# A decoder layer with a state-space scan: the products with C issued a step later, their consumers behind the next scan, the carries a step sooner

## The chip, the cores and the metric

The kernel runs on one core of a Trainium2 chip, in one launch. The metric is the device time of that core in microseconds, the median of a few runs. The engines are named as in the profile: PE multiplies matrices, DVE (VectorE) and ACT (ScalarE) work element by element, POOL is GpSimd, and SP only issues DMAs here.

## What is computed

One decoder layer on 8 sequences of 512 positions with 512 features: a Mamba block, an attention block on a second input, and a mixture of 32 experts, each followed by a residual and a layer norm. The part that the change touches is the Mamba block's recurrence. Cut to that part, the reference reads:

```python
xz = xn @ in_proj_w                                   # 512 -> 2 x 1024
x_main, z = jnp.split(xz, 2, axis=-1)
x_main = silu(causal_depthwise_conv1d(x_main))
dt, B_ssm, C_ssm = jnp.split(x_main @ x_proj_w, [32, 48], axis=-1)
dt = softplus(dt @ dt_proj_w + dt_proj_b)
dA  = exp(A * dt[..., None])                          # A = -exp(A_log), 1024 x 16 states
dBx = dt[..., None] * B_ssm * x_main[..., None]
h_t = dA_t * h_{t-1} + dBx_t                          # for every t, channel and state
y_t = sum over the 16 states of h_t * C_t
y   = (y + x_main * D_param) * silu(z)
out = res_scale * (y @ out_proj_w) + residual
```

After it come a layer norm, cross attention with 16 heads of 32 features, another norm, a router that picks 4 of 32 experts in groups, the experts with a capacity of 640 tokens each, a shared expert, a scatter-add and a last norm.

## The kernel before

**Stages.** `layers` does the Mamba and attention blocks, the routing and the shared expert; `experts` runs the 32 experts; `finish` does the last norm. The change lies in `layers`, which fills the profile up to about 3690 us.

**Chunks and steps.** The 8 sequences are cut into chunks of T = 256 positions, so there are 16 chunks, two to a sequence. A chunk has 32 steps, numbered k: four pairs q of blocks of 128 channels, and in each pair four groups g of 4 states, times the two blocks of the pair (ci). There are 512 steps in all. One step handles 128 channels, 4 states and 256 positions, laid out as a tile `h` of 128 x 4 x 257: the first column of each of the four stretches is the carry from the chunk before.

**What one step does.** `carry` (L452, ACT) takes a new `h` and copies the carries into it. `decays` (L446, ACT) makes the four 128x256 pieces of exp(A dt) in one of two buffers `das`, one step ahead. `scan` multiplies dt·x by B into `h` (L458, DVE), runs the recurrence in place (L462, DVE) and keeps the last column (L464, DVE). `collect` multiplies `h` by C in place (L479, DVE), and then PE sums over the states: four matmuls (L483) for each step into the PSUM tile `py`, behind two matmuls at the first group (L471) that put x·D there. When the 8 steps of a pair are done, `gated` (L495, DVE) multiplies `py` into silu(z).

**Buffers.** `h` has 4 buffers, so step k+4 reuses the memory of step k and has to wait until PE has read it. `py` has one. The broadcast rows of B and C come by DMA from a scratch tensor (`bcast`, six tiles `bc`). `prepare` makes dt and dt·x of the next pair: its last DVE instruction, L421, is followed by DMAs on SP's queue that spread the result into the tiles `both`, which the first L458 of the pair waits for.

**Work beside the scan.** In the same loop stand, at fixed k, the projection back of the chunk before (`back`, L512), the projection of z (`gate_x`, L311), its `silu` (L362, each with a change of ACT's function table), and for the next chunk the norm, the convolution (`convolve`, taps at L345), `x_proj` and `prepare`. The list `side` holds the attention, the routing and the shared expert of the sequence before, in pieces that are taken out as the planned work allows (`work`). Attention's scores (L775), their maxima (L777, DVE), the transposed scores (L801), the exponentials (L805, ACT) and the sums with V (L817) are the bulk of it.

**What sets the order.** No queue is written out by hand. Python traces the instructions in the loop's order, and the framework's scheduler then orders each engine's queue: among the instructions that its own model holds for ready it takes those traced first. The place of a call in the loop is thus a priority and not a position. Once a queue is built, its order is fixed. `do` and `settle` put the second part of a piece (the evacuation of its PSUM tile) behind the next piece.

The loop's lines around the change, before:

```python
h = carry(t, 2 * q + ci, g)
...
    decays(2 * nq + ni, ng, (f if k + 1 < len(steps) else nf)["ready", nq][0], das[(n + 1) % 2])
scan(t, 2 * q + ci, g, f["ready", q][1], bc, das[n % 2], h)
n += 1
if k % 8 == 0:
    if k:
        gated(q - 1, f, py)
...
settle()
collect(2 * q + ci, g, h, bc, py, f)
```

Of the kernel before, what the change touches and what calls it, by code (L numbers as in the profile page):

```python
# [8 lines left out]
F32 = mybir.dt.float32  # L9
# [3 lines left out]
ALU = mybir.AluOpType  # L13
# [4 lines left out]
P = 128  # L18
# [6 lines left out]
NST = 16  # L25
RANK = 32
CC = DI // P
T = 256
NT_ = T // P
NG = 4  # L30
HP = P // 2
# [51 lines left out]
def layers(ctx, tc, a, x1d, filld, based, xbuf):  # L83
# [23 lines left out]
    nc = tc.nc  # L107
# [11 lines left out]
    psy = ctx.enter_context(tc.tile_pool(name="l_psy", bufs=1, space=PSUM))  # L119
# [3 lines left out]
    ident = cp.tile([P, P], F32, name="l_ident")  # L123
    make_identity(nc, ident)

    twice = cp.tile([P, HP], F32, name="l_twice")
# [92 lines left out]
    first = cp.tile([P, E], F32, name="l_first")  # L219
    nc.gpsimd.iota(first, pattern=[[CAP, E]], base=-SLOTS, channel_multiplier=0, allow_small_or_imprecise_dtypes=True)  # L220
    first = first.unsqueeze(1).to_broadcast([P, SC, E])
# [158 lines left out]
    def bcast(f, g):  # L380

        got = []
        for r0 in (g * NG, NST + g * NG):
            t = bcp.tile([P, NG // 2, T], F32, tag="bc", name="bc")
            for r in range(2):
                n0 = r0 + r * NG // 2
                nc.sync.dma_start(
                    t[r * HP : (r + 1) * HP], f["scr"][n0 : n0 + NG // 2, :].partition_broadcast(HP)
                )
            got.append(t.unsqueeze(1).to_broadcast([P, 2, NG // 2, T]))  # L390
        return got
# [50 lines left out]
    def decays(c, g, dt, da):  # L442

        for n in range(NG):
            j, m = n // 2, n % 2
            nc.scalar.activation(da[:, n, 1:], dt[:, c % 2, j, :], AF.Exp, scale=aneg[:, c, j, g, m : m + 1])  # L446

    def carry(t, c, g):

        last = state[:, c, g].unsqueeze(2)  # L450
        h = mp.tile([P, NG, T + 1], F32, tag="h", name="h", bufs=4)
        nc.scalar.copy(h[:, :, 0:1], last if t else nothing)  # L452
        return h

    def scan(t, c, g, dtx, bc, da, h):

        steps = h.rearrange("p (j m) t -> p j m t", j=2)[:, :, :, 1:]
        nc.vector.tensor_tensor(  # L458
            steps, dtx[:, c % 2].unsqueeze(2).to_broadcast([P, 2, NG // 2, T]), bc[0], ALU.mult
        )  # L460
        flat = h.rearrange("p n t -> p (n t)")
        nc.vector.tensor_tensor_scan(flat, da.rearrange("p n t -> p (n t)"), flat, 0.0, ALU.mult, ALU.add)  # L462
        if t < S // T - 1:
            nc.vector.tensor_copy(state[:, c, g].unsqueeze(2), h[:, :, T : T + 1])  # L464

    def collect(c, g, h, bc, py, f):


        if g == 0:
            for j in range(2):  # L470
                nc.tensor.matmul(  # L471
                    py[j * HP : (j + 1) * HP, c % 2, :],
                    ident[:, j * HP : (j + 1) * HP],
                    f["xs"][c // 2][:, c % 2, :],
                    start=(c % 2 == 0),
                    stop=False,
                )
        steps = h.rearrange("p (j m) t -> p j m t", j=2)[:, :, :, 1:]
        nc.vector.tensor_tensor(steps, steps, bc[1], ALU.mult)  # L479
        for m in range(NG // 2):  # L480
            for j in range(2):
                s = (g, m, c % 2)
                nc.tensor.matmul(  # L483
                    py[j * HP : (j + 1) * HP, c % 2, :],
                    twice,
                    h[:, j * 2 + m, 1:],
                    start=False,
                    stop=(s == (NST // NG - 1, NG // 2 - 1, 1)),
                )

    def gated(q, f, py):

        f["xs"].pop(q)
        pair = f["zs"][:, 2 * q : 2 * q + 2, :]
        nc.vector.tensor_tensor(pair, pair, py, ALU.mult)  # L495

    def twice_x(b, t, f):
        f["o"] = o = mp.tile([P, NT_, D], F32, tag="xt", name="o")
        nc.sync.dma_start(o, a["x"][b, t * T : (t + 1) * T, :].rearrange("(j p) d -> p j d", p=P))
        nc.scalar.mul(o, o, 2.0)  # L500
# [501 lines left out]
    steps = [(q, g, i) for q in range(CC // 2) for g in range(NST // NG) for i in range(2)]  # L1002
    left = []

    def settle():

        got = [part() for part in left]
        left[:] = [x for x in got if x]

    def dry():  # L1010
        while left:
            settle()

    def do(fn, *args, first=False):

        if first:
            dry()
        rest = fn(*args)
        settle()
        if rest:  # L1020
            left.append(rest)

    def work(k):

        front = 6.9 if k in (1, 2) else 3.4 if 3 <= k < 7 or k in (12, 15, 18, 21, 24) else 1.0 if k in (11, 26) else 0.0
        return 1.2 + front

    f = {"xt": x0}
# [12 lines left out]
    bc, n = bcast(f, 0), 0  # L1041
    nc.scalar.activation(aneg, aneg, AF.Exp)
    nc.vector.tensor_scalar(aneg, aneg, -1.0, None, ALU.mult)
    decays(0, 0, f["ready", 0][0], das[0])
    old, side, cleared = None, [], 0

    for i, (b, t) in enumerate(chunks):
        nf = {}
        after = chunks[i + 1] if i + 1 < len(chunks) else None
        if t == 0:  # L1050
            side, spent = units(b - 1) if b else sources(0), 0.0

            own = [work(k) for k in range(len(steps))] * 2
            whole = sum(own) + sum(x[0] for x in side)
        py = None
        for k, (q, g, ci) in enumerate(steps):
            if ci == 0:
                if (q, g) != (CC // 2 - 1, NST // NG - 1):
                    bcn = bcast(f, (g + 1) % (NST // NG))
                else:  # L1060
                    bcn = bcast(nf, 0) if after else None
            h = carry(t, 2 * q + ci, g)

            if k + 1 < len(steps) or after:
                nq, ng, ni = steps[(k + 1) % len(steps)]
                decays(2 * nq + ni, ng, (f if k + 1 < len(steps) else nf)["ready", nq][0], das[(n + 1) % 2])
            scan(t, 2 * q + ci, g, f["ready", q][1], bc, das[n % 2], h)
            n += 1
            if k % 8 == 0:
                if k:  # L1070
                    gated(q - 1, f, py)
                elif old:
                    gated(CC // 2 - 1, old[2], old[3])
                py = psy.tile([P, 2, T], F32, tag="py", name="py")
            if i == 0 and k == 0:
                load("Wo")
            if i == 0 and k == 2:
                biases()
            if k == 0 and old:
                twice_x(*old[:3])  # L1080
            if k in (1, 2) and old:
                do(back, k - 1, *old[:3], first=True)
            if 3 <= k < 7:
                do(gate_x, k - 3, f, first=(k == 3))
            if k == 7:
                dry()
                silu(f["zs"])
            if k % 8 == 3:
                if q + 1 < CC // 2:
                    do(prepare, q + 1, f)  # L1090
                elif after:
                    do(prepare, 0, nf)
            if after:
                if k == 5:
                    load_x(*after, nf)
                if k == 9:
                    norm_x(nf)
                if k == 11:
                    for j in range(DC // 2):
                        do(flip_x, j, nf)  # L1100
                if k in (12, 15, 18, 21):
                    do(convolve, after[1], (k - 12) // 3, nf, first=(k == 12))
                if k == 23:
                    dry()
                    silu(*nf["xs"].values())
                if k == 24:
                    do(x_proj, nf)
            if side and (k >= 3 or t and k == 0):
                at = t * len(steps) + k + 1
                while side and spent + sum(own[:at]) <= whole * at / len(own):  # L1110
                    w, fn, alone = side.pop(0)
                    spent += w
                    do(fn, first=alone)
            settle()
            collect(2 * q + ci, g, h, bc, py, f)
            if ci == 1:
                bc = bcn
            while i < 2 and cleared < E * (i * len(steps) + k - 6) // (2 * len(steps) - 7):
                clear(cleared)
                cleared += 1  # L1120
        while t and side:
            _, fn, alone = side.pop(0)
            do(fn, first=alone)
        old = (b, t, f, py)
        f = nf
    gated(CC // 2 - 1, old[2], old[3])
    twice_x(*old[:3])
    for j in range(2):
        do(back, j, *old[:3], first=True)
    dry()  # L1130
    for _, fn, alone in units(B - 1):
        do(fn, first=alone)
# [347 lines left out]
```

## Time and profile before

| what | value |
|---|---|
| median of 3 runs | 5548.85 us (5548.56 to 5548.85) |
| the profiled execution: time, span | 5555.79 us, 5554.1 us |
| PE, DVE, ACT, POOL busy, share of the span | 88%, 78%, 47%, 10% |
| mean granted TensorE clock | 0.936 |
| steps of the scan | 512, from 54 to 3685 us |
| L462, the recurrence | 512 x 2291 ns |
| L458 and L479, the products with B and C | 512 x 1213 ns and 512 x 1218 ns |

The profiled execution took 5555.79 us, of which the instructions span 5554.1 us; it lies 6.9 us (0.12%) above the median. In the page's rows a line number is followed by the engine, the operation, the tile written and the tiles read, the number of instructions, the busy time in us with the mean of one in ns, and behind the second bar the time for which the engine stood idle just before such instructions, with the instruction that ended most of it. In the list of waits a row names who waited for whom, with the total in us, the number of waits and the longest.

### The profile page before, as it was taken

How to read it: one execution, taken by the hardware profiler on the slowest of the kernel's cores; microseconds unless marked ns; L12 is line 12 of the kernel's file. 1: busy time of each engine (PE TensorE's matmuls, PEld its weight loads, DVE VectorE, ACT ScalarE, POOL GpSimd, SP SyncE). 2: the span in 40 equal slices, each digit the busy share in tenths (PEclk: the TensorE clock that was granted, in tenths of full speed). 3: DMA queues.
4: the chain of work that ended last, by engine and by line, in shares of the span. 5: the costliest groups of instructions: out<-in, count | busy, mean ns of one | idle time of the engine just before them, and what ended most of it. 6: DMA issues, size and time to landing. Idle time of an engine off the chain costs nothing. (4 is left out here: it accounts for less than half of the span.)

```text
span 5554.1 us, 60352 instructions
## 1 busy us (share of the span) xinstructions
PE 4883.9 (88%) x19752; PEld 2720.5 (49%) x19752; DVE 4349.2 (78%) x5738; ACT 2592.8 (47%) x5483; POOL 560.9 (10%) x424
## 2 busy tenths in 40 slices
PE   6768889888988988888888898879899999999994
PEld 3334344334434434443443343333577777777773
DVE  7998989989889989899989999864466565555554
ACT  5554565655556555555555655523222222222223
POOL 1000002002000200200010020010111111111111
PEclk7878999999999999999999999989999999999997
DMA  6887345445534634544463464441345444454444
GB/s 183 246 239 203 108 130 184 114 120 154 167 104 113 203 92 129 184 123 113 124 199 104 114 193 110 113 157 44 102 121 125 125 125 124 121 126 124 115 121 146
DMA packets 554282, 769.83 MB, mean 139 GB/s; under 512 B 135754, under 2 KB 268394, under 8 KB 551920
## 3 DMA queue, kind: packets, MB, share of 16 engines
q1 hardware_dynamic: 517952, 677.55, 41.5%
q0 software_dynamic: 33280, 76.90, 7.3%
q10 hardware_dynamic: 2736, 11.54, 0.5%
q8 instruction: 156, 2.56, 0.2%
q14 instruction: 158, 1.29, 0.1%
HBM read 508.68 MB, written 165.05 MB: 121 GB/s over the span
## 5 line engine op out<-in xcount | busy, mean ns | idle before, releaser
L446 ACT ACTIVATE l_da<-both,l_aneg 128x256 f32<-128x256 f32 x2048 | 888.7, 499 | 791.5 <-DVE h L462 744.2
L462 DVE TENSOR_TENSOR_SCAN h<-l_da,h 128x1028 f32<-128x1028 f32 x512 | 1169.4, 2291 | 49.9 <-ACT h L452 27.3
L483 PE MATMUL py<-h,l_twice 128*64 128x256 f32 x4096 | 632.0, 424 | 194.2 <-DVE h L479 194.0
L458 DVE TENSOR_TENSOR h<-both,bc 128x1024 f32<-128x1024 f32 x512 | 617.5, 1213 | 141.8 <-PE py L483 78.2
L479 DVE TENSOR_TENSOR h<-h,bc 128x1024 f32<-128x1024 f32 x512 | 621.9, 1218 | 6.3 <-DMA l_qa<-l_ka 0.3
L483 PEld LDWEIGHTS py<-h,l_twice 128*64 128x64 f32 x4096 | 295.2, 148 | 570.5 <-issue 246.4
L775 PE MATMUL ps_s<-l_ka,l_qa 64*128 64x512 f32 x1024 | 315.2, 695 | 141.9 <-DVE mx L777 141.4
L1230 PE MATMUL ps_h<-xT,w 128*128 128x320 f32 x1536 | 435.6, 433 | 0.0
L1310 POOL DMA_INDIRECT based<-y,xe x160 | 251.2, 1570 | 1313.4 <-ACT y L1333 573.4
L1251 DVE TENSOR_TENSOR hT<-ps_h,p 128x320 f32<-128x320 f32 x128 | 62.9, 491 | 379.1 <-PE ps_h L1230 379.1
L777 DVE TENSOR_REDUCE mx<-ps_s 128x2 f32<-128x1024 f32 x256 | 310.2, 1215 | 56.2 <-PE ps_s L775 55.5
L1230 PEld LDWEIGHTS ps_h<-xT,w 128*128 128x128 f32 x1536 | 292.2, 190 | 118.2 <-issue 0.4
L801 PE MATMUL ps_t<-l_qa,l_ka 64*128 64x512 f32 x1024 | 300.6, 651 | 15.0 <-ACT eT L805 11.4
L805 ACT ACTIVATE eT<-ps_t 128x1024 f32<-128x1024 f32 x256 | 258.7, 1012 | 109.2 <-PE ps_t L801 108.7
L817 PE MATMUL po<-eT,l_va 128*64 128x512 f32 x1024 | 281.5, 628 | 24.6 <-ACT raw L829 20.8
L650 POOL DMA_INDIRECT xbuf<-x2t,dest x128 | 218.7, 1708 | 815.8 <-DVE dest L644 777.4
L1230 PE MATMUL ps_h<-t,s 128*128 128x320 f32 x1024 | 286.1, 432 | 0.0
L712 PE MATMUL ps_p<-x2T,wa 128*128 128x512 f32 x512 | 247.5, 633 | 11.8 <-DVE hT L892 10.3
L311 PE MATMUL ps_z<-xnT,wm 128*128 128x256 f32 x1024 | 241.0, 389 | 17.8 <-DVE o L521 17.0
L311 PE MATMUL ps_x<-xnT,wm 128*128 128x256 f32 x1024 | 242.5, 390 | 2.9 <-DMA wm<-in_in_proj_w 2.0
L512 PE MATMUL po<-wm,zs 128*128 128x512 f32 x512 | 234.6, 608 | 3.9 <-DMA wm<-in_out_proj_w 1.8
L1230 PEld LDWEIGHTS ps_h<-t,s 128*128 128x128 f32 x1024 | 194.6, 190 | 81.1
(234 smaller groups left out, 7414.6 us busy)
## 6 DMA issues: line engine op xcount, KB each, us to landing
bc<-scr SPq DMA_DIRECT2D x1024, 128.0 KB
w<-in_w SPq DMA_DIRECT2D x93, 1024.0 KB
wm<-in_in_proj_w SPq DMA_DIRECT2D x128, 512.0 KB
xbuf<-zero SPq DMA_DIRECT2D x32, 1362.5 KB
xe<-xbuf SPq DMA_DIRECT2D x32, 1362.5 KB
both<-dt SPq DMA_DIRECT2D x256, 128.0 KB
both<-dtx SPq DMA_DIRECT2D x256, 128.0 KB
wm<-in_out_proj_w SPq DMA_DIRECT2D x64, 512.0 KB
```

The lines of the kernel that those rows point to most:

```text
L311: nc.tensor.matmul(ps[:, i, :], w[:, dc, i * P : (i + 1) * P], f["xnT"][:, dc, :], start=(dc == 0), stop=(dc == DC - 1),)
L446: nc.scalar.activation(da[:, n, 1:], dt[:, c % 2, j, :], AF.Exp, scale=aneg[:, c, j, g, m : m + 1])
L458: nc.vector.tensor_tensor(steps, dtx[:, c % 2].unsqueeze(2).to_broadcast([P, 2, NG // 2, T]), bc[0], ALU.mult)
L462: nc.vector.tensor_tensor_scan(flat, da.rearrange("p n t -> p (n t)"), flat, 0.0, ALU.mult, ALU.add)
L479: nc.vector.tensor_tensor(steps, steps, bc[1], ALU.mult)
L483: nc.tensor.matmul(py[j * HP : (j + 1) * HP, c % 2, :], twice, h[:, j * 2 + m, 1:], start=False, stop=(s == (NST // NG - 1, NG // 2 - 1, 1)),)
L775: nc.tensor.matmul(ps[:, j, :], qa[r, lt * P : (lt + 1) * P], ka[r, :], start=True, stop=True)
L777: return lambda: nc.vector.tensor_reduce(mx[:, lt, :].unsqueeze(2), ps, AX.X, ALU.max) and None
L801: nc.tensor.matmul(ps[:, j, :], ka[r, kc * P : (kc + 1) * P], qa[r, :], start=True, stop=True)
L805: nc.scalar.activation(eT, ps, AF.Exp)
L817: nc.tensor.matmul(po[j * 2 * HD : (j + 1) * 2 * HD, :], va[:, kc, i, j * HD : (j + 2) * HD], eT[:, j, :], start=(kc == 0), stop=(kc == SC ...
L1230: nc.tensor.matmul(ps, w[:, n, r * P : (r + 1) * P], x[:, n, :], start=not more and n == 0, stop=n == 1, skip_group_check=more,)
```

## The change

`collect` now does only the multiplication with C (L469) and returns a function `products`, which the loop calls one step later, ahead of the next step's `collect`. With it goes the allocation of `py`, which the first products of a pair now make. `carry` of step k+1 is called in step k, ahead of the decays of step k+1. `gated` moves from the first to the second step of the next pair, `back` from k = 1, 2 to 2, 3, `gate_x` from 3..6 to 4..7, the `silu` of z from 7 to 8, and `side` may begin a step later. A `settle` is called right behind the scan and its consumers, in place of the one just ahead of `collect`. After the last chunk the last `products` are called ahead of the last `gated`. Nothing else is changed: same tiles, same buffers, same instructions, apart from what the scheduler makes of them. In the new file L489 are the products, L479 the two x·D matmuls, L469 the multiplication with C and L503 `gated`.

```diff
-    def collect(c, g, h, bc, py, f):
-        if g == 0:
-            for j in range(2):
-                nc.tensor.matmul(py[...], ident[...], f["xs"][c // 2][:, c % 2, :], ...)
+    def collect(c, g, h, bc, f):
         steps = h.rearrange("p (j m) t -> p j m t", j=2)[:, :, :, 1:]
         nc.vector.tensor_tensor(steps, steps, bc[1], ALU.mult)
-        for m in range(NG // 2):
-            for j in range(2):
-                nc.tensor.matmul(py[...], twice, h[:, j * 2 + m, 1:], ...)
+        xs = f["xs"][c // 2]
+
+        def products():
+            if g == 0 and c % 2 == 0:
+                f["py"] = psy.tile([P, 2, T], F32, tag="py", name="py")
+            py = f["py"]
+            if g == 0:
+                for j in range(2):
+                    nc.tensor.matmul(py[...], ident[...], xs[:, c % 2, :], ...)
+            for m in range(NG // 2):
+                for j in range(2):
+                    nc.tensor.matmul(py[...], twice, h[:, j * 2 + m, 1:], ...)
+
+        return products
...
-            h = carry(t, 2 * q + ci, g)
+            h = ahead
             if k + 1 < len(steps) or after:
                 nq, ng, ni = steps[(k + 1) % len(steps)]
+                ahead = carry(t if k + 1 < len(steps) else after[1], 2 * nq + ni, ng)
                 decays(2 * nq + ni, ng, ...)
             scan(t, 2 * q + ci, g, f["ready", q][1], bc, das[n % 2], h)
             n += 1
-            if k % 8 == 0:
-                if k:
-                    gated(q - 1, f, py)
+            if k % 8 == 1:
+                if k > 1:
+                    gated(q - 1, f)
                 elif old:
-                    gated(CC // 2 - 1, old[2], old[3])
-                py = psy.tile([P, 2, T], F32, tag="py", name="py")
+                    gated(CC // 2 - 1, old[2])
...
-            if k in (1, 2) and old:
-                do(back, k - 1, *old[:3], first=True)
-            if 3 <= k < 7:
-                do(gate_x, k - 3, f, first=(k == 3))
-            if k == 7:
+            settle()
+            if k in (2, 3) and old:
+                do(back, k - 2, *old, first=True)
+            if 4 <= k < 8:
+                do(gate_x, k - 4, f, first=(k == 4))
+            if k == 8:
                 dry()
                 silu(f["zs"])
...
-            if side and (k >= 3 or t and k == 0):
+            if side and (k >= 4 or t and k < 2):
...
-            settle()
-            collect(2 * q + ci, g, h, bc, py, f)
+            if products:
+                products()
+            products = collect(2 * q + ci, g, h, bc, f)
```

More of the change, by code (lines that the diff above doesn't have):

```diff
@@ L464, in scan, with gated @@
             nc.vector.tensor_copy(state[:, c, g].unsqueeze(2), h[:, :, T : T + 1])
-    def collect(c, g, h, bc, py, f):
-        if g == 0:
-            for j in range(2):
[L471 to L477, printed above, removed]
+    def collect(c, g, h, bc, f):
         steps = h.rearrange("p (j m) t -> p j m t", j=2)[:, :, :, 1:]
         nc.vector.tensor_tensor(steps, steps, bc[1], ALU.mult)
-        for m in range(NG // 2):
-            for j in range(2):
[L482 to L491, printed above, removed]
+        xs = f["xs"][c // 2]
[5 more added lines that the diff above has]
+                for j in range(2):
+                    nc.tensor.matmul(
+                        py[j * HP : (j + 1) * HP, c % 2, :],
+                        ident[:, j * HP : (j + 1) * HP],
+                        xs[:, c % 2, :],
+                        start=(c % 2 == 0),
+                        stop=False,
+                    )
+            for m in range(NG // 2):
+                for j in range(2):
+                    s = (g, m, c % 2)
+                    nc.tensor.matmul(
+                        py[j * HP : (j + 1) * HP, c % 2, :],
+                        twice,
+                        h[:, j * 2 + m, 1:],
+                        start=False,
+                        stop=(s == (NST // NG - 1, NG // 2 - 1, 1)),
+                    )
+        return products
+    def gated(q, f):
         f["xs"].pop(q)
         pair = f["zs"][:, 2 * q : 2 * q + 2, :]
-        nc.vector.tensor_tensor(pair, pair, py, ALU.mult)
+        nc.vector.tensor_tensor(pair, pair, f["py"], ALU.mult)
     def twice_x(b, t, f):
@@ L1023, in work @@
     def work(k):
-        front = 6.9 if k in (1, 2) else 3.4 if 3 <= k < 7 or k in (12, 15, 18, 21, 24) else 1.0 if k in (11, 26) else 0.0
+        front = 6.9 if k in (2, 3) else 3.4 if 4 <= k < 8 or k in (12, 15, 18, 21, 24) else 1.0 if k in (11, 26) else 0.0
         return 1.2 + front
@@ L1044, in layers @@
     decays(0, 0, f["ready", 0][0], das[0])
+    ahead, products = carry(0, 0, 0), None
     old, side, cleared = None, [], 0
@@ L1054, in layers @@
             whole = sum(own) + sum(x[0] for x in side)
-        py = None
         for k, (q, g, ci) in enumerate(steps):
@@ L1079, in layers @@
             if k == 0 and old:
-                twice_x(*old[:3])
-            if k in (1, 2) and old:
-                do(back, k - 1, *old[:3], first=True)
-            if 3 <= k < 7:
-                do(gate_x, k - 3, f, first=(k == 3))
-            if k == 7:
+                twice_x(*old)
+            settle()
[4 more added lines that the diff above has]
+            if k == 8:
                 dry()
@@ L1123, in layers @@
             do(fn, first=alone)
-        old = (b, t, f, py)
+        old = (b, t, f)
         f = nf
-    gated(CC // 2 - 1, old[2], old[3])
-    twice_x(*old[:3])
+    products()
+    gated(CC // 2 - 1, old[2])
+    twice_x(*old)
     for j in range(2):
-        do(back, j, *old[:3], first=True)
+        do(back, j, *old, first=True)
     dry()
```

## The prediction

> **What bounds the kernel now.** I read the page's table of engines first, then a window over the steady part of the scan, then the list of waits, then the order of time around one wait.
>
> ```profile
> PE 4883.9 (88%) x19752; PEld 2720.5 (49%) x19752; DVE 4349.2 (78%) x5738; ACT 2592.8 (47%) x5483; POOL 560.9 (10%) x424
> 139.00:3600.00 3461.00, 2972.29 (x12178) 1411.87 (x12178) 3142.33 (x3570) 1963.59 (x4174) 259.60 (x189) 0.93 0.51 148
> ```
>
> The second line (length; then busy time of PE, PE's loads, DVE, ACT, POOL) is the stage that the change touches. DVE is busy for 3142.3 of 3461 us, 91%, so 319 us is all that better order could give there. PE shows 86% and ACT 57%. What ends DVE's idle time, and whom PE's products keep waiting:
>
> ```profile
> DVE h L458 <- PE py L483: 78.2, 33, 5.2
> DVE h L458 <- DMA both<-dtx: 47.9, 21, 6.9
> DVE xs L345 <- ACT xs L337: 43.7, 25, 9.8
> DVE h L462 <- ACT h L452: 27.3, 15, 2.0
> DVE zs L495 <- PE py L483: 23.9, 17, 2.4
> PE py L483 <- DVE h L479: 194.0, 58, 9.1
> ACT h L452 <- PE py L483: 199.4, 137, 6.9
> ```
>
> The largest idle time of DVE in the scan is L458 waiting for products: the buffer of `h` that step k+4 wants is still being read for step k. One such place in order of time:
>
> ```profile
> 2418.97 7.03 PE L712 MATMUL ps_p<-x1T,wa 128*128 128x512 f32 x16
> ...
> 2425.93 1.08 PE L483 MATMUL py<-h,l_twice 128*64 128x256 f32 x8
> ...
> 2427.06 1.23 DVE L458 TENSOR_TENSOR h<-both,bc 128x1024 f32<-128x1024 f32 x1 [3.42 <-PE py L483]
> ```
>
> PE's queue holds 7 us of attention's projections ahead of the products; the products follow at 2425.93 and DVE, which has stood for 3.42 us, goes on as they end. So the products are not late because their input is late: they are late because of what is queued ahead of them.
>
> **What the Trainium skill says.** "Perfetto Trace Analysis", section Optimization Strategy, says that the same gap coming back on the engine that should be saturated can mean too few buffers. The trace agrees: this wait of 3 to 5 us comes back at the same two steps in every pair of chunks (at 2338.8 and 2427.1 us, and 469 us earlier at 1870.0 and 1956.7). The section on the Tensor Engine Instruction of that page says that DVE and ACT are strict FIFO: whatever stands behind a waiting L458 or a waiting carry waits too; the 3.42 us above is bare idle time. "ScalarE: Activation LUTs", section What ACT_TABLE_LOAD costs, gives 1283 ns for a load and 1380 ns for a drain with it; the trace has 1283 ns, and 1.0 us of idle time before the 61 loads of L362 together, so I price a load at 1.28 us alone.
>
> **The change, part by part.** No matmul, DMA or vector instruction of the loop is added or taken away. The order of the built queues, before and after, tells what the scheduler does with the new places.
>
> *Products a step later.* Each is traced behind the next step's scan and side work, so PE's queue puts more ahead of them. I counted for each of the first 508 steps how many multiplications with C of later steps PE's queue needs done before it gets to this step's products: none, one, two, three. Before: 205, 167, 129, 7. After: 209, 124, 155, 20. Two or more rise from 136 to 175, with four buffers as before. What that costs, as an estimate from the trace's durations: take the last DVE instruction that PE's queue needs up to step k's products, the DVE work from there to L458 of step k+4 (rows: 1.213, 2.291, 1.218 us, 1.215 for L777, others by their size), and subtract PE's work from the same point through the products (intervals between back-to-back matmuls: 0.29 us a product, 0.46 a 128x256, 0.96 a 128x512, 0.55 an attention matmul). Where this is below zero the buffer can't be free in time. Before, 27 steps are, 34.1 us in sum, and the trace has 19 of its waits and 57 of its 78.2 us just there, so the count finds the places. After, 75 are, 79.7 us in sum. The ratio is 2.34. Of neighbouring steps only the worst should pay, since a stall also gives PE time: with one payment for adjacent steps it is 57.1 over 31.5, 1.81; with one for steps up to four apart 48.0 over 31.5, 1.52. I take 1.81: 78.2 us become 141.5, **+63 us**, between +41 and +105. Most of it should stand in one run of steps, the second to seventh of the second chunk of a sequence, where `back` and `gate_x` sit on PE.
>
> *Less waiting on PE.* What the move could bring is the 194 us in which the products stand at the head of PE's queue waiting for L479, with attention behind them. But the steps whose own multiplication is the latest thing PE needs are 128 before and 130 after. I take **0**; the bounds are -60 (a third of it, if it all reached DVE) and 0.
>
> *Carries a step sooner.* They need the same buffer, which now comes free later. Carries that stand ahead of their own step's decays on ACT rise from 151 to 181, and behind a waiting carry ACT's decays, exponentials and evacuations wait. ACT is idle for 43% of the stage, which hides most. I scale L462's wait for it, 27.3 us, by 181/151: **+5**, between -27 (all of it gone) and +25.
>
> *dt·x of the next pair.* The scheduler, not an edit, moves L421 further ahead of the pair's first L458. At the second pair of a chunk the DVE work between them, 1.3 us before, becomes 5.0 and 1.2 in turn; at the third 5.0 and 7.8 become 8.0 and 13.9; at the fourth 8.7 and 5.7 become 12.6 and 9.0. In order of time the 47.9 us split into 30.1 at the second pair, 6.8, 6.9 and 4.1 at the others. Half of the first and both of the next go: **-29**, between -44 and 0. SP's queue issues the same DMAs and isn't waited for.
>
> *`gated` a step later*, on DVE behind the next scan: its wait of 23.9 us gets some 5 us more for the last products, which are themselves later. **-10**, between -24 and +5. The next pair's first products wait for it on PE (`py` is one buffer; L471 waits 14.9 us now): both move by one step, 0, between -15 and +10.
>
> *`back`, `gate_x`, `silu`, `side` a step later.* Same work; `silu` stays one step ahead of its reader. Loads of ACT's tables fall from 138 to 98, 40 x 1.28 = 51 us, since the scheduler no longer splits the silu calls around an exponential. ACT isn't full, so what shows is L462's wait for decays (8.3 us) and the taps' (43.7): **-5**, between -25 and 0. The first chunk and the tail after the last one see the same instructions: 0; were its cover gone, a step's products are 1.1 us.
>
> The sum is 63 + 0 + 5 - 29 - 10 - 5 = +24 us, 0.43%. On the profiled execution, 5555.8 us, that is 5580; it stood 6.9 us above the median, and on the median of 5548.85 it is **5573 us**.
>
> **The rivals.** (a) *The products' full price.* DVE pays every deficit (+105), and the carries, held by the same buffers, stop ACT for another 25: with 15 us left of the gains, +115 us, 5664. For it speaks that ACT's carries already wait 199.4 us for PE; against it that stalls relieve each other. (b) *Faster: PE runs free.* The 194 us on PE's queue shrink. The counts of what DVE owes to PE go that way for other matmuls: the scores' matmuls (L775), which wait for the maxima (141.4 us of PE's idle time), are pressed in 80 places instead of 126 by the same kind of count. If PE gains about 60 us through this, its deficits of 1 us a step dissolve: the products' extra +63 doesn't come, and with -29, -10, -5 and some -15 of the old 78.2 us it is -59, 5490. It decides when PE is ahead by more than a microsecond at most of the 75 places; against it stand the 128 and 130. (c) *The change doesn't do what it says.* The scheduler re-forms nearly the same queues, the counts are scatter, gains and losses cancel: 5549.
>
> **How the numbers follow.** The measurement can tell about 0.2%, 11 us, from no change. The forecast, slower by some 24 us (its own range 5562 to 5612), has a chance of 0.43; rival (a) 0.10; (b) 0.31; (c) 0.16. So faster 0.31, same 0.16, slower 0.53. The range reaches from (b) to short of (a): 5490 to 5645.
>
> **What would show it.** Right: L458's wait for the products (L489) grows from 78 us to 110 to 180 and stands at more steps; its wait for `both` falls under 30 us; ACT shows 98 loads; DVE's busy time in the scan is unchanged and its idle time grows. Wrong: L458's wait is at or under 78 us, or PE's wait of products for L469 falls far under 194 us and the scores' with it, and the scan ends before 3690 us. An equal time with a smaller buffer wait would mean that another wait took its place, ACT's carries first.

## The result and the profile after

The changed kernel takes 5606.39 us (median of 4 runs, 5602.28 to 5612.04) against 5548.85: 57.5 us more, a ratio of 1.0102 with a 95% interval of 1.0085 to 1.0120. The direction was forecast, at less than half the size (24 us). The profiled execution took 5602.28 us with a span of 5600.6, 46.5 us over the span of before. It is the shortest of the four runs while the profiled one of before lay above its median, so the traces hold 46.5 of the 57.5 us.

The page's engine line and the same window of the scan as before (length; busy PE, PE's loads, DVE, ACT, POOL):

```profile
PE 4884.3 (87%) x19752; PEld 2727.5 (49%) x19752; DVE 4358.2 (78%) x5738; ACT 2535.0 (45%) x5443; POOL 541.5 (10%) x424
139.00:3600.00 3461.00, 2926.92 (x11960) 1400.62 (x11962) 3101.95 (x3533) 1873.12 (x4065) 238.53 (x189) 0.93 0.51 146
```

The work of the whole kernel is the same for PE and DVE; in the window DVE is busy for 3102 us instead of 3142 and so idle for 359 instead of 319, and PE does 45 us less there. Taken step by step, the last recurrence starts at 3736.3 us instead of 3680.6: 55.7 us are lost inside the scan, and the part behind it is 9.2 us shorter: DVE has 29 instructions, 7.4 us, less to do there, so some of that work is now done earlier. ACT has 40 instructions less, the table loads that fell from 138 to 98 as counted.

The list of DVE's waits after (who for whom: us in total, times, longest):

```profile
DVE h L458 <- PE py L489: 108.8, 77, 5.3
DVE mx L785 <- PE ps_s L783: 76.1, 47, 2.8
...
DVE xs L345 <- ACT xs L337: 49.1, 34, 10.7
DVE h L458 <- DMA both<-dtx: 39.0, 9, 8.6
...
DVE h L462 <- ACT h L452: 31.6, 20, 3.9
DVE g_m L567 <- ACT g_sc L566: 27.7, 7, 5.4
...
DVE zs L503 <- ACT zs L362: 17.2, 6, 2.9
...
DVE zs L503 <- PE py L489: 10.1, 5, 3.0
```

And from the list of all waits, what ACT and PE waited for:

```profile
ACT h L452 <- PE py L489: 247.7, 129, 11.5
...
PE py L489 <- DVE h L469: 189.9, 57, 8.9
PE ps_s L783 <- DVE mx L785: 187.5, 92, 4.8
```

No single row holds 57 us. The wait for products rose by 30.6 us (78.2 to 108.8), the maxima's wait for the scores by 20.6 (55.5 to 76.1), a wait for the router's exponential is all but new (0.4 to 27.7), `gated` waits 9.0 more for silu (8.2 to 17.2) and 13.8 less for products (23.9 to 10.1), the wait for dt·x fell by 8.9 (47.9 to 39.0). PE's waits for the multiplication with C are what they were (194.0 and 189.9).

### The profile page after: what moved, and what is told of

Read it like the earlier page. It is cut to its first block, busy times and chain, and to the rows that moved or that the text cites. A ratio compares the mean times of both kernels' runs of the same rounds, so it can differ in the third digit from the quotient of the medians.

```text
span 5600.6 us, 60350 instructions
## 1 busy us (share of the span) xinstructions
PE 4884.3 (87%) x19752; PEld 2727.5 (49%) x19752; DVE 4358.2 (78%) x5738; ACT 2535.0 (45%) x5443; POOL 541.5 (10%) x424
## 3 DMA queue, kind: packets, MB, share of 16 engines
q14 instruction: 159, 1.29, 0.1%
## 5 line engine op out<-in xcount | busy, mean ns | idle before, releaser
L462 DVE TENSOR_TENSOR_SCAN h<-l_da,h 128x1028 f32<-128x1028 f32 x512 | 1168.8, 2292 | 50.9 <-ACT h L452 31.6
L489 PE MATMUL py<-h,l_twice 128*64 128x256 f32 x4096 | 656.0, 427 | 189.9 <-DVE h L469 189.9
L458 DVE TENSOR_TENSOR h<-both,bc 128x1024 f32<-128x1024 f32 x512 | 618.6, 1216 | 154.7 <-PE py L489 108.8
L469 DVE TENSOR_TENSOR h<-h,bc 128x1024 f32<-128x1024 f32 x512 | 621.7, 1218 | 6.8
L489 PEld LDWEIGHTS py<-h,l_twice 128*64 128x64 f32 x4096 | 303.4, 148 | 559.6 <-issue 233.5
L783 PE MATMUL ps_s<-l_ka,l_qa 64*128 64x512 f32 x1024 | 306.4, 665 | 187.9 <-DVE mx L785 187.5
L785 DVE TENSOR_REDUCE mx<-ps_s 128x2 f32<-128x1024 f32 x256 | 310.5, 1216 | 77.5 <-PE ps_s L783 76.1
L658 POOL DMA_INDIRECT xbuf<-x2t,dest x128 | 205.8, 1608 | 782.0 <-DVE dest L652 697.1
L783 PEld LDWEIGHTS ps_s<-l_ka,l_qa 64*128 64x128 f32 x1024 | 85.2, 191 | 343.0 <-DVE mx L785 281.2
```

Of the source, the lines that this page charges most:

```text
L458: nc.vector.tensor_tensor(steps, dtx[:, c % 2].unsqueeze(2).to_broadcast([P, 2, NG // 2, T]), bc[0], ALU.mult)
L489: nc.tensor.matmul(py[j * HP : (j + 1) * HP, c % 2, :], twice, h[:, j * 2 + m, 1:], start=False, stop=(s == (NST // NG - 1, NG // 2 - 1, 1)),)
L783: nc.tensor.matmul(ps[:, j, :], qa[r, lt * P : (lt + 1) * P], ka[r, :], start=True, stop=True)
L785: return lambda: nc.vector.tensor_reduce(mx[:, lt, :].unsqueeze(2), ps, AX.X, ALU.max) and None
```

## The experiments

**Products alone: nothing to run.** A kernel of before in which only the products are issued a step later (behind the next scan, ahead of `gated`) was built. Its queues are those of before on every engine, instruction by instruction: the scheduler puts the products where it put them already. So at that place the first clause of the change does nothing, and its effect needn't be measured. In the changed kernel the products stand further back in the loop, ahead of the next `collect` and so behind that step's pieces; that place by itself, with the `gated` that it forces a step later, was not measured.

**Carries alone.** `carry_only` is the kernel before with one edit:

```diff
-            h = carry(t, 2 * q + ci, g)
+            h = ahead
...
+                ahead = carry(t if k + 1 < len(steps) else after[1], 2 * nq + ni, ng)
                 decays(...)
```

> The kernel before with the carries alone a step sooner. PE's queue stays as it was; only ACT's order changes, at 328 places. Theory A (buffers of h, of which the sooner carries are a part): L462's wait for carries grows from 27 us by about 5, time +5 us (0.1%). Theory B (the moved consumers make the loss): no change that can be measured, within 0.2%. Theory C (carries that wait for a buffer hold up ACT's exponentials): +20 us or more, with L462's wait for L452 at 50 us or over.

Measured 5555.7 us, ratio 1.0007 [1.0000, 1.0014]; DVE's wait for the carries is 23.5 us. The other way round, the changed kernel without this edit:

> The changed kernel with the carries back at their own step. Theory A and B: within 0.2% of the changed kernel, 5595 to 5615 us, L462's wait for carries at 25 to 35 us. Theory C (carries): 20 us or more faster than the changed kernel.

Measured 5603.93 us, ratio 1.0101 [1.0084, 1.0118], the time of the changed kernel; the wait for carries falls to 7.5 us and the wait for products rises to 134.2. The 24.1 us that go from the one wait come back as 25.4 in the other: the carries decide in which row the waiting shows, and they don't set the time. Theory C falls.

**The moved consumers alone.** `consumers_only` moves `back`, `gate_x`, `side` and the settle, and leaves products, `gated`, silu and carries. With the pieces goes their weight in `work`, the plan by which `side` is dealt out; the changed kernel has that shift too, though the diff further up leaves the line out:

```diff
-            if k in (1, 2) and old:
-                do(back, k - 1, ...)
-            if 3 <= k < 7:
-                do(gate_x, k - 3, ...)
+            settle()
+            if k in (2, 3) and old:
+                do(back, k - 2, ...)
+            if 4 <= k < 8:
+                do(gate_x, k - 4, ...)
...
-            if side and (k >= 3 or t and k == 0):
+            if side and (k >= 4 or t and k < 2):
...
-            settle()
             collect(...)
```

> The kernel before with only back, gate_x and side a step later (and the settle behind the scan); products, gated, silu and carries stay where they were. Theory A (the products' own delay makes the loss): within 0.3% of before. Theory B (the moved consumers): the larger part of the +57 us of the whole change, 30 us or more, with new waits of DVE for the router's exponential (L566 of the changed kernel; about 27 us) and for the scores, and the wait of L458 for products over 78 us at the steps just behind the moved pieces.

Measured 5661.86 us, 1.0205 [1.0188, 1.0222]: about twice the loss of the whole change. Theory B holds on the time, but not in its detail: the wait for the router isn't there and the wait for products is at its old size (75.0 us); what grew most is the wait for dt·x, which was 47.9 us:

```profile
DVE h L458 <- DMA both<-dtx: 93.6, 20, 8.9
```

The carries set no time, so the other edits of the change (products, `gated` and silu a step later) take away about 55 us of what the moved consumers cost. Which of the three does so was not tried; together they are a gain beside the moved pieces, where the prediction had its largest loss.

**A fifth buffer.** `after_h5` is the changed kernel with `bufs=5` for `h`; the router's `g_any`, `g_gs` and `g_rank` share memory with its other tiles to make room.

> The changed kernel with five buffers of h in place of four; three small router tiles share memory to make room. Theory A (buffers are what L458 waits for): its wait for products falls from 109 us under 40 us and the time falls by 40 us or more, near or below the kernel before. Rival: the scheduler uses the fifth buffer to put still more ahead of the products (steps whose products stand behind three or more later multiplications rise from 20 to 144), so the wait stays near 100 us and the time within 20 us of the changed kernel.

Measured 5606.18 us, 1.0098 [1.0081, 1.0115], equal to the changed kernel. DVE's two largest waits of L458:

```profile
DVE h L458 <- DMA both<-dtx: 107.8, 19, 8.8
DVE h L458 <- PE py L489: 95.0, 56, 4.4
```

The rival holds: the wait for products stays near 100 us, the one for dt·x grows from 39.0 to 107.8, and the time is the same. Theory A, which is the prediction's view that the loss is one of buffers of `h`, is not borne out. The scheduler made new queues for five buffers; what a fifth would do in unchanged queues isn't shown.

**Which consumer.** Three kernels move one piece each, on the kernel before: `back` alone, `gate_x` alone (each with its weights in `work`), the settle alone; and one is the changed kernel with `back` at its old k = 1, 2.

> The kernel before with back alone a step later (k = 2, 3), with its weights in the plan. Theory D (back is the piece whose move costs, since its 16 matmuls now come together with prepare of the next pair and stand ahead of products): +25 us or more, with more waits of L458 for products or for both. Theory E (no single piece: gate_x, side and back cost only together): within 0.3% of before.

> The kernel before with gate_x alone a step later (k = 4 to 7), with its weights in the plan. Theory D (back is the piece): within 0.3% of before, L458's wait for products at or under 78 us. Rival (gate_x is the piece, behind prepare of the next pair): +25 us or more, with L458's wait for both over 80 us.

> The kernel before with only the settle moved from just ahead of collect to just behind the scan's consumers. ACT's table loads fall from 138 to 87, 65 us of ACT. Theory (ACT is off the path): within 0.2% of before. Rival (ACT's order holds DVE up at silu and the taps): 15 us or more faster. Theory E' (the settle makes the loss of consumers_only): 25 us or more slower.

> The changed kernel with back at its old steps, k = 1, 2. Theory D (back): the loss is gone for the most part, 5550 to 5580 us. Theory E (the pieces cost together, or another one carries it): within 0.3% of the changed kernel, 5590 to 5620 us.

Measured: `back_only` 5618.53 us, 1.0121 [1.0104, 1.0138]; `gate_only` 5556.47, 1.0006 [0.9997, 1.0014]; `settle_only` 5586.42, 1.0054 [1.0037, 1.0071]; `after_back` 5571.38, 1.0035 [1.0022, 1.0047]. So theory D holds for the most part: `back` costs, and `gate_x` doesn't. About a third of the changed kernel's loss is left when `back` is put back, and the settle alone costs about half as much as the whole change, in spite of 51 table loads less (138 to 87), which bring nothing that shows. In `after_back` only the call of `back` moves; the plan in `work` and the steps that are closed to `side` (k = 2, 3) stay as in the changed kernel. With `back` at its old place the wait for products is less than half of what it was in the changed kernel:

```profile
DVE mx L785 <- PE ps_s L783: 94.5, 61, 3.2
...
DVE h L458 <- PE py L489: 50.1, 59, 6.3
```

**Both put back, and the four combinations.** `after_settle` is the changed kernel with the settle ahead of the products again, `after_back_settle`, whose edit is shown, has `back` at k = 1, 2 as well:

```diff
-            settle()
-            if k in (2, 3) and old:
-                do(back, k - 2, *old, first=True)
+            if k in (1, 2) and old:
+                do(back, k - 1, *old, first=True)
...
+            settle()
             if products:
                 products()
```

> The changed kernel with back at its old steps and the settle at its old place. If the settle carries what is left of the loss (it cost 33 us alone), the time falls from 5571 to 5540 to 5560 us, level with the kernel before; if not, it stays within 0.3% of 5571.

> The changed kernel with only the settle at its old place. If settle and back add up, 30 us under the changed kernel, 5565 to 5585 us, and DVE's wait for the router's exponential is gone; if settle costs only in company with back's old place, within 0.2% of 5606.

| changed kernel, ratio to before | `back` at 2, 3 | `back` at 1, 2 |
|---|---|---|
| settle behind the scan's consumers | 1.0102 [1.0085, 1.0120] | 1.0035 [1.0022, 1.0047] |
| settle ahead of the products | 1.0046 [1.0028, 1.0064] | 0.9973 [0.9963, 0.9984] |

`back`'s place costs 0.67% in one row and 0.73% in the other, the settle's 0.56% and 0.62%: they add up, to 1.29%, and everything else in the change gains 0.27% (0.16 to 0.37). `after_back_settle`, at 5541.62 us, is faster than both kernels; its products are a step later, and L458 waits for them for 53.1 us, less than the 78.2 of before.

These prices hold in the changed kernel. In the kernel before, `back` alone costs 1.21%, and it does so by other waits:

```profile
DVE h L458 <- PE py L483: 99.5, 66, 3.9
DVE xs L345 <- ACT xs L337: 97.9, 39, 9.2
```

The convolution's taps wait for ACT 54 us longer there than before (43.7), and the wait that the account below is about isn't there: at the fifth and sixth steps of the second chunks L458 waits for no products at all. Why the move of `back` alone does that is open; what follows holds for the changed kernel.

**Why `back` costs there.** First the changed kernel in order of time, at one of those places (start, length, engine, line, tiles; in brackets the idle time and what ended it):

```profile
2111.01 1.22 DVE L785 TENSOR_REDUCE mx<-ps_s 128x2 f32<-128x1024 f32 x1
...
2112.34 7.13 PE L520 MATMUL po<-wm,zs 128*128 128x512 f32 x16
...
2112.46 1.23 DVE L458 TENSOR_TENSOR h<-both,bc 128x1024 f32<-128x1024 f32 x1 [0.22 <-PE py L489]
...
2113.79 2.30 DVE L462 TENSOR_TENSOR_SCAN h<-l_da,h 128x1028 f32<-128x1028 f32 x1
...
2116.12 1.23 DVE L469 TENSOR_TENSOR h<-h,bc 128x1024 f32<-128x1024 f32 x1
...
2119.89 1.03 PE L489 MATMUL py<-h,l_twice 128*64 128x256 f32 x8
2120.85 0.70 PE L520 MATMUL po<-wm,zs 128*128 128x512 f32 x1
...
2120.97 1.22 DVE L458 TENSOR_TENSOR h<-both,bc 128x1024 f32<-128x1024 f32 x1 [3.62 <-PE py L489]
```

A half of `back` is 7.13 us on PE. In the step beside it DVE has its own L458, L462 and L469 and nothing else, done 4.9 us after they began; then it stands for 3.62 us until PE has done the half and the products behind it. The next half follows at 2120.85. With `back` a step earlier, in `after_back`, the first half runs beside attention's work on DVE:

```profile
2089.27 7.13 PE L520 MATMUL po<-wm,zs 128*128 128x512 f32 x16
...
2089.98 0.69 DVE L856 TENSOR_TENSOR total<-total,r 128x512 f32<-128x512 f32 x1
...
2090.70 0.69 DVE L857 SCALAR_TENSOR_TENSOR total<-total,r 128x512 f32<-128x512 f32 x1
...
2091.43 0.69 DVE L858 SCALAR_TENSOR_TENSOR attT<-attT,total 128x512 f32<-128x512 f32 x1
...
2092.04 0.68 DVE L503 TENSOR_TENSOR zs<-zs,py 128x512 f32<-128x512 f32 x1
...
2092.64 1.22 DVE L458 TENSOR_TENSOR h<-both,bc 128x1024 f32<-128x1024 f32 x1
```

Here DVE has L856 to L858 and `gated` (L503) beside its scan for the time in which PE is taken up, and its L458 starts without a wait. In the kernel before, the queues put the same pieces of attention (there L848 to L850) beside the first half, and the wait behind it is short:

```profile
2081.60 7.13 PE L512 MATMUL po<-wm,zs 128*128 128x512 f32 x16
...
2082.26 0.69 DVE L848 TENSOR_TENSOR total<-total,r 128x512 f32<-128x512 f32 x1 [0.56 <-ACT r L847]
...
2090.23 1.22 DVE L458 TENSOR_TENSOR h<-both,bc 128x1024 f32<-128x1024 f32 x1 [1.03 <-PE py L483]
```

The place shown is one of seven, one in each second chunk from the second sequence on, always at the sixth step (k = 5). These seven waits sum to 28.2 us in the changed kernel, 3.5 before and nothing in `after_back`. Two more places follow `back`: the fifth step of the same chunks has 8.6 us (1.6 in `after_back`), and the eighth step of the first chunks 32.2 (13.8). Of the 53.6 us that so go, 18.4 come back as the maxima's wait for the scores (76.1 to 94.5); the times differ by 35.

The reading was tested by making the halves shorter, with the places kept. Both kernels leave out half of the matmuls:

```diff
-                for i in range(2):
+                for i in range(1):
                     c = 2 * q + i
                     nc.tensor.matmul(pos[j], yg[:, c, ...], w[:, i, :], ...)
```

> The kernel before with half of back's matmuls left out (8 of 16 in a chunk; the projection back then sums only half of the channels). It is the measure for the next kernel. PE loses 113 us of work; if PE is not the bound where back stands before, the time falls by under 25 us (the waits for products just behind back, 24 us).

> The changed kernel with the same half of back's matmuls left out. Theory F (back's 7.1 us halves are longer than the DVE work of the steps where they stand now, so PE sets the pace there): the loss against the same kernel before shrinks from 57 us to under 25 us, and L458's wait for products falls from 109 us under 60 us. Rival (what was moved upsets the order as such, however long the matmuls are): the loss stays at 40 us or more.

Measured 5509.29 us for the kernel before (0.9923 [0.9907, 0.9940]) and 5522.04 for the changed one (0.9947 [0.9930, 0.9964]): 12.8 us apart where the full kernels are 57.5. The wait for products is 47.3 and 52.8 us. At the place that was shown, DVE has the same three instructions beside the shorter half, and its wait behind it is a quarter of what it was:

```profile
2078.07 4.43 PE L520 MATMUL po<-wm,zs 128*128 128x512 f32 x8
...
2084.00 1.23 DVE L458 TENSOR_TENSOR h<-both,bc 128x1024 f32<-128x1024 f32 x1 [0.92 <-PE py L489]
```

The seven waits of the sixth step fall from 28.2 to 3.3 us. So theory F holds: at these places it is the length of `back` on PE against the DVE work beside it. Whether as much PE work taken away elsewhere would have brought the two kernels as near to each other was not tried. The expectation for the kernel before missed: it gained 46 us (0.77%; the kernel before stood at 5555.45 us beside it), not under 25, so PE sets the pace in places there too.

**What the settle costs.** In the changed kernel, the wait that comes with the moved settle and goes with the old one is DVE's for the router's exponential (27.7 us, and 0.4 in `after_settle`). Two kernels tried it alone, and one both edits with it:

> The changed kernel with the router's work behind its exponential as a part of its own, behind the next piece. If that wait (27 us) is on the path, the time falls by 15 to 30 us and the rest of the settle's cost is small; if it covers another wait, the time stays within 0.2% of 5606.

> The changed kernel without the router's exponential (its scores are then ranked as plain differences, so other experts are picked; the sizes of all work stay the same). Theory (the wait for it is on the path and is the settle's part of the loss): DVE's 27 us wait is gone and the time falls by 18 to 30 us against the changed kernel, to 5576 to 5590 us. Rival (it covers other waits): within 0.2% of 5606 us, with L458's and the scores' waits grown by some 25 us.

> The same, and the router's work behind its exponential becomes a part of its own, behind the next piece. Theory (DVE's 24 us of waiting for that exponential are on the path): that wait is gone and the time is 10 to 25 us under that of the kernel without this edit. Rival (the wait covers another one, PE's): it goes, and waits for the scores grow by as much, the time the same within 0.2%.

Measured 5602.49 us (1.0094 [1.0076, 1.0113]), 5599.21 us (1.0090 [1.0073, 1.0107]) and 5538.31 us (0.9973 [0.9961, 0.9986]). In `after_router` the wait stayed in the queue (25.6 us in the scan), so that run tells nothing of it; in `after_back_settle` it was gone (0.4 us) before the edit was made, so the third doesn't either. In `after_noexp` it is gone, and 15.3 us of waiting for PE (L899, which takes up the result of a projection) are new; the gain against the changed kernel, some 7 us, is not clear of its interval. Nor can that wait be the settle's price everywhere: `settle_only` is 0.54% slower with 0.4 us of it. There it is `gated`'s wait for the products that grew most, from 23.9 us:

```profile
DVE zs L495 <- PE py L483: 51.6, 23, 4.4
```

The settle's cost is shown as an edit; by which wait it reaches the time stays open.

## Why the prediction was wrong in size

**What held.** The kernel became slower, and the wait for products grew where it was said to: in the second to seventh step of a sequence's second chunk the order of time has 51.7 us after 15.3, and that is more than the whole growth. The reading that the products are late for what PE's queue holds ahead of them, and not for their input, holds too. The carries were put at +5 us, and `carry_only` measured 0.07%, 4 us, with [0.00, 0.14]%. PE's wait for the multiplication with C was put at no gain: 194.0 became 189.9. Loads of tables fell to 98. Rival (b) is out, since the kernel is slower; its sign fails as well: the scores' waits on PE rose, 141.4 to 187.5 us, where its count had let them fall.

**That the direction was right is luck in part.** Without the 63 us for the products, the sum is a gain of 39. The loss came from edits that the sum had at -5 and at nothing.

**The step that failed is "`back`, `gate_x`, `silu`, `side` a step later. Same work", priced at -5.** The work is the same, but not the work beside it. In the changed kernel the first half of `back` stands, in seven of the eight second chunks, in a step where DVE has only the scan (the wait behind it is 28.2 us in sum, 3.5 before), and the move costs 0.7% (about 39 us); the settle, which the prediction gave no price at all, costs 0.6% (about 33 us). With those two put back, the change is a gain of 0.27%. Through which wait the settle costs, and why the moved pieces cost more without the rest of the change, stays open.

**The products' term was mis-sized and put down to the wrong edit.** 63 us were forecast for "products a step later" through the buffers of `h`; the wait grew by 30.6, to just under the 110 to 180 us named for it. With `back` at its old place it is 50.1 us, and with the settle put back too 53.1, while the products are a step later in both; and the fifth buffer changes no time. The count told where DVE would stand, and not what puts it there: since the pieces' places had not been undone one by one in the queues, the products got the blame. Which edits raised the count from 27 to 75 was not counted apart. The prediction also names no loss at the eighth step of the first chunk, where 32.2 us of the wait stand; 24.4 stood there before.

**Smaller terms.** dt·x: -29 forecast, the wait fell by 8.9; the second pair of the first chunk came free (13.5 us to none), but at the second pair of the second chunk, left with 1.2 us of cover, 16.6 became 34.6, and no rise was forecast anywhere. `gated`: -10 forecast; -13.8 for the products, but 9.0 more for silu. The maxima's (+20.6) and the router's (+27.7) waits stood nowhere in the sum. DVE's waits are no independent terms: where one is taken away (the carries, the exponential), another comes in its place.

## What to carry to other kernels

Where a scheduler makes the queues, build each part of a change alone, at the place that it takes in the whole, and compare the queues before pricing it: a part may do nothing, and another that looks like mere tidying may move everything. A long piece on one engine belongs beside a stretch where the other engine has work of its own; a step's move is then worth the difference between the two stretches, even where no instruction is added. And a buffer that one engine waits for is not yet the bound: ask what stands ahead of its release, and try one buffer more.

## What had not been expected

Fewer changes of ACT's table brought nothing: 138 to 87 loads, 65 us of ACT, in a kernel that was 0.54% slower for the settle's sake. And PE, at 86% busy against DVE's 91% in the scan, is near enough to the bound that leaving out half of `back`, 103 us of PE's busy time in the traces, shortened the kernel before by 46 us.
